# Another order of the background work in the scans of two Mamba layers

## The chip, the cores and the metric

The kernel runs on one core of one Trainium2 chip. The metric is the device time of one execution in microseconds; the median of three runs is given. The core has five engines, each with a queue of its own that it works off in order: TensorE (PE, matmuls into PSUM), VectorE (DVE), ScalarE (ACT, functions from tables that have to be loaded), GpSimd (POOL), and SyncE (SP), which here issues the DMAs.

## The reference

Four images go through four layers with residual connections. Two are attention layers, which the change doesn't touch. The third is a Mamba layer, the fourth a grouped Mamba layer with an MLP. What the last two compute, cut to what matters:

```python
# Mamba: xn is the normalised input, B=4, L=4096, D_INNER=512, 16 states
xi, z = split(xn @ in_proj.T)
u     = silu(causal_conv4(xi) + conv_b)
dt, Bm, Cm = split(u @ x_proj.T)                 # "x_proj"
delta = softplus(dt @ dt_proj + dt_proj_b)       # "delta"
h_t   = exp(delta_t * A) * h_{t-1} + (delta_t * u_t) * B_t     # 16 states
y_t   = sum_n h_t[n] * C_t[n]
out   = ((y + u * D) * silu(z)) @ out_proj.T

# grouped layer: the 256 channels in 4 groups of 64, each its own Mamba (128 inner channels,
# shared weights); then for every group
m = ln(mamba(group)); m = gelu(m @ fc1 + b1) @ fc2 + b2 + skip * group     # "MLP"
y = silu(batchnorm(outc @ concat(m)))                                       # "out_conv", "out_silu"
```

## The kernel before, in words

The images are worked off one after the other, the layers of an image too. A Mamba layer's 4096 time steps are cut into four chunks (k) of 1024. In a chunk there are four blocks of 128 inner channels. For the Mamba layer these are the blocks d = 0 to 3. For the grouped layer they are the four groups, taken as two pairs (c = 0, 1); the pair's first block is `even`, its second `odd`. A block has 16 slots, one for each state n. So a layer has 256 slots.

`scan_blocks` writes out, slot by slot, what each engine gets. In slot i:

- VectorE multiplies `du` with the spread B (L913, tile `pb`) and runs the scan (L919, `h`).
- GpSimd multiplies h with C (L925, `hc`). Two slots ahead it makes the product `du*B` (L830, `bb`) for "apart" slots, in which VectorE then doesn't multiply. Apart are slots 0, 4, 8 of a grouped block and 0, 5, 10 of a Mamba block. B for them comes by DMA, loaded four slots ahead.
- ScalarE makes exp(delta*A) three slots ahead (L856, `da`; for apart slots `dap` two slots ahead, into PSUM) and keeps the state (L861).
- TensorE spreads B over the partitions two slots ahead (L844, `pb`) and adds up y by transposes (L872, `y`) for the slot before.
- In between come the slot's background steps, `blk["bg"][n]`, in the order in which `put` filed them.

On TensorE the background of slot i stands ahead of the spread for slot i+2 and of the transposes of slot i-1. On VectorE it stands behind the scan of slot i, on GpSimd behind `hc` of slot i, on ScalarE behind `da` for slot i+3. What waits in the background thus holds up what stands behind it on its engine.

The background prepares what later blocks need, in the grouped layer:

- `x_proj` (`table_steps`): two projections with their evictions (x0, x1: L1623, L1072; behind the second the DMAs that store B and C), then four steps that split the table into two bf16 parts: a cast on ScalarE (L1080), a subtraction of 64 rows on GpSimd ("r64", L1083), a second cast, a subtraction of 32 rows ("r32"). The steps are numbered 0 to 5. For the Mamba layer each projection is two steps (0 to 3), and the parts are 4 to 7.
- `delta` (`delta_steps`): matmul and three functions on ScalarE (softplus, L1040 to L1044), an add on VectorE (L1048), the same for the second half, then `times_u` on GpSimd (L1052, `du`).
- `norm`: mean, center (L979), deviation (L990, L953), scale (GpSimd, L996), affine (ScalarE, L1003) for each half of the next chunk.
- `mlp`: out_proj (L1638), deviation (L1648), scale (GpSimd, L1653), hidden(0) (L1659), fc1 (gelu with two table loads, L1666, and hidden(1)), fc2(0), fc2(1) (L1682, L1687). m0 and m1 are the two halves of the pair before.
- `out_conv` (L1707, L1713), `out_silu`, `out` (GpSimd add L1732 and DMA); `all_u` (L1570) and `silu` (L1602, two table loads) make u for the next pair; `in_z` makes z.

All these matmuls share a PSUM pool, "mm", of two banks; hidden takes both. `end` finishes a block in slots 1 to 3 of the next one (L883 copy of y, L893 and L897 `fin_ps`, L886). Lists named `late` pass steps on to the next pair; what is left after the last pair runs behind the scan, in the tail, ahead of the last pair's MLP.

For the Mamba layer the change concerns the last block (d = 3) of each chunk but the last, in which u's last quarter, x_proj and the first delta of the next chunk are made.

Of the kernel before, what the change touches and what calls it, by code (L numbers as in the profile page):

```python
# [45 lines left out]
class Net:  # L46
# [1065 lines left out]
    def mamba_layer(self, x, bridge, pe_dram, w_in, w_cw, w_x, w_dt, w_out, v_dram):  # L1112
        tc, nc = self.tc, self.nc
        ND = 4
        with ExitStack() as ctx:
# [226 lines left out]
            for k in range(n_chunk):  # L1342
# [28 lines left out]
                if more:  # L1371

                    if k == 0:
                        put(0, (0,), (lambda: begin(1),))
                        put(0, (0, 0, 1, 3, 4, 5, 6, 7), self.later(lambda: norm(1, 0), 8))
                    h1 = self.later(lambda k=k: norm(k + 1, 1), 8)
                    if k:
                        put(0, (2, 4, 5, 7, 8, 13, 14, 15), h1)
                    else:
                        put(0, (7, 8, 9, 12, 13, 14, 15), h1[:7])  # L1380
                        put(1, (1,), h1[7:])
                    if k + 2 < n_chunk:
                        put(3, (3,), (lambda k=k: begin(k + 2),))
                        h0 = self.later(lambda k=k: norm(k + 2, 0), 8)
                        put(3, (4, 6, 7, 14, 15), h0[:5])
                        chunks[k + 1]["late"] = ((0, 1, 2), h0[5:])
                    if k:
                        put(0, *chunks[k]["late"])
                    u = all_u(k + 1)
                    put(1, range(5, 16), u[:11])  # L1390
                    put(2, range(14), u[11:25])
                    put(3, (1, 2, 3, 4, 5, 5, 6), u[25:])
                    xs = x_proj(k + 1)
                    put(2, (13,), (silu((k + 1, 0, "u"), (k + 1, 1, "u"), (k + 1, 2, "u"),
                                        (k, 2, "zs")),))
                    put(3, (7,), (silu((k + 1, 3, "u"), (k, 3, "zs")),))
                    put(3, (7, 8, 8, 9, 9, 10, 11, 12), xs)
                    put(3, (9, 10, 10, 11, 12), delta(k + 1, 0))
                else:
                    put(2, (13,), (silu((k, 2, "zs"), (k, 3, "zs")),))  # L1400

                    sums, about, square, squares, early_squares = stats

                    def square_into(i):
                        tag, bufs = ("pe", 1) if i % 2 else ("u", 5)
                        square(i, work.tile([P, NC], F32, tag=tag, name="cs_sq", bufs=bufs))

                    for i in range(6):
                        put(1 + (13 + i) // DS, ((13 + i) % DS,), (lambda i=i: sums(i),))
                        put(2 + (12 + i) // DS, ((12 + i) % DS,), (lambda i=i: square_into(i),))  # L1410
                        put(2 + (13 + i) // DS, ((13 + i) % DS,), (lambda i=i: squares(i),))
                    put(2, (3,), (about,))
                    put(3, (3,), (early_squares,))
                    for i in range(4):
                        at = (6 + 2 * i, 7 + 2 * i)
                        put(3, at, out_proj(k, i // 2, i % 2, ((0, 1, 2),)))
# [70 lines left out]
    def grouped_mamba_layer(self, x, bridge, begun, ws_dram, outc_dram, v_dram, out_b):  # L1487
        tc, nc = self.tc, self.nc
        w_in, w_cw, w_x, w_dt, w_out, w_f1, w_f2 = ws_dram
        with ExitStack() as ctx:  # L1490
# [136 lines left out]
            def delta(k, q):  # L1627
                return self.delta_steps(chunks[k]["blocks"][q], wdt, work, psum)
# [188 lines left out]
            for i, (k, c) in enumerate(pairs):  # L1817
# [12 lines left out]
                if more:  # L1830
                    h0, h1 = (self.later(lambda k=k, s=s: norm(k + 1, s), 5) for s in range(2))
                    put(even, (0,), (lambda k=k: begin(k + 1),))
                    put(even, (0, 1, 4, 5, 6), h0)
                    put(even, (14, 15), h1)
                    put(odd, (1, 2, 3), h1[2:])
                put(even, (4, 5, 6, 7, 8, 9), x_proj(k, 2 * c + 1))
                if i:
                    m0, m1 = mlp(*pairs[i - 1], 0), mlp(*pairs[i - 1], 1)
                    put(even, (5, 6, 7, 10, 11, 12, 13), m0)
                    put(even, (6, 7, 8), m1)  # L1840
                    if c == 0:
                        put(even, (14, 15), m1[3:])
                        put(odd, (0, 1), m1[5:])
                    else:
                        put(odd, (15,), m1[3:])
                        late.append(((0, 1, 1), m1[4:]))
                put(even, (7, 8, 8, 9, 10), delta(k, 2 * c + 1))
                also = [lambda k=k: out_silu(k - 1)] if c == 1 and k else []
                if i == 0:
                    put(even, (0,), xs0[5:])  # L1850
# [6 lines left out]
                if c == 1 and k:  # L1857
                    put(even, (4, 4, 5, 5), [out(k - 1, *sm) for sm in outs])
                if c == 0 and k:
                    put(odd, (10, 12, 15), [out_conv(k - 1, *sm) for sm in outs[:3]])  # L1860
                    late.append(((0,), [out_conv(k - 1, *outs[3])]))

                if i + 1 < len(pairs):
                    nk, ncol = pairs[i + 1]
                    put(odd, (4, 5, 6, 7), all_u(nk, ncol))
                    put(odd, (7,), (silu(nk, ncol, "u"),))
                    put(odd, (8, 8, 8, 9, 10, 11), x_proj(nk, 2 * ncol))
                    put(odd, (9, 10, 10, 11, 12), delta(nk, 2 * ncol))
                    put(odd, (13, 14), [in_z(nk, ncol, s) for s in range(2)])
            self.scan_blocks(  # L1870
                [blk for c in chunks for blk in c["blocks"]], loop, psum, psb, psy, (0, 4, 8),
# [125 lines left out]
```

## Time and profile before

| what | us |
|---|---|
| median of 3 runs (lowest to highest) | 12572.97 (12561.93 to 12574.42) |
| the profiled execution: device time, span | 12578.04, 12576.3 |
| Mamba scan, second image | 968.9 |
| between the two scans | 58.8 |
| grouped scan, second image | 980.9 |
| tail behind it, to the end of the image | 56.4 |
| busy over the whole span: PE, DVE, ACT, POOL | 10378.1, 10244.0, 7241.3, 9022.1 |

An image is some 3140 us: two attention layers (about 1080), the Mamba scan, the grouped scan. In the rows of a time line the columns are start, length, engine, line, operation, out<-in, shapes and count; the bracket at the end is the idle time of the engine just before, and what ended it. In rows of groups the columns behind the bar are busy us and mean ns of one, then idle us before them with what ended it.

### The profile page before, as it was taken

The numbers are of one execution on the slowest core, as the hardware profiler recorded it, in microseconds if no ns is written. First come the engines' busy times: TensorE is split into PE (matmuls) and PEld (weight loads), VectorE is DVE, ScalarE is ACT, GpSimd is POOL, SyncE is SP. The second block draws the span as 40 slices with busy tenths as digits, with TensorE's granted clock in tenths as the row PEclk, the third lists the DMA queues.
The fourth block names the chain that finished last, engine by engine and source line by source line (L and its number), as shares of the span: only waits on it lengthen the run. The fifth ranks groups of instructions, "written<-read, shape, count | busy, mean of one in ns | idle before, by whom it ended". The sixth has DMA issues, their size and how long they took to land. (4 is left out here: it accounts for less than half of the span.)

```text
span 12576.3 us, 159645 instructions
## 1 busy us (share of the span) xinstructions
PE 10378.1 (83%) x54656; PEld 6079.4 (48%) x54656; DVE 10244.0 (81%) x9074; ACT 7241.3 (58%) x13292; POOL 9022.1 (72%) x4634
## 2 busy tenths in 40 slices
PE   8987887777898788778789878877778987887787
PEld 4664444443466454444446645444434664444443
DVE  6778997887677899798767789978976778997897
ACT  4565554776456555477646655547764565554776
POOL 4666886887466688688746668868874666886887
PEclk9998998998899899899889989989988998998998
DMA  3343444554334455455433445445543344554554
GB/s 96 106 130 129 171 168 137 168 169 141 98 107 126 132 169 169 137 170 169 141 98 108 127 133 170 168 137 169 169 141 97 107 128 131 171 168 138 169 168 142
DMA packets 687147, 1782.94 MB, mean 142 GB/s; under 512 B 89856, under 2 KB 197888, under 8 KB 685312
## 3 DMA queue, kind: packets, MB, share of 16 engines
q1 hardware_dynamic: 686336, 1772.74, 43.6%
q8 instruction: 435, 7.13, 0.2%
q14 instruction: 376, 3.08, 0.1%
HBM read 1610.91 MB, written 94.37 MB: 136 GB/s over the span
## 5 line engine op out<-in xcount | busy, mean ns | idle before, releaser
L925 POOL TENSOR_TENSOR hc<-h,cb 128x1024 f32<-128x1024 f32 x2056 | 4817.5, 2351 | 1099.0 <-DVE h L919 502.8
L919 DVE TENSOR_TENSOR_SCAN h<-da,m_state,pb 128x1024 f32<-128x1024 f32 x1248 | 2920.4, 2340 | 162.0 <-DVE pb L913 1.9
L872 PE MATMUL y<-ident,hc 128*128 128x128 f32 x16384 | 2378.0, 294 | 313.7 <-POOL hc L925 211.4
L872 PEld LDWEIGHTS y<-ident,hc 128*128 128x128 f32 x16384 | 2098.8, 152 | 979.4 <-POOL hc L925 374.5
L913 DVE TENSOR_TENSOR pb<-du,pb 128x1024 f32<-128x1024 f32 x1672 | 2025.8, 1212 | 147.3 <-PE pb L844 98.8
L856 ACT ACTIVATE da<-delta,m_v 128x1024 f32<-128x1024 f32 x1672 | 1899.1, 1141 | 215.9 <-DVE h L919 205.4
L844 PE MATMUL pb<-m_parts,pick 128*128 128x512 bf16 x3280 | 1082.2, 414 | 896.9 <-DVE h L919 893.7
L502 ACT ACTIVATE pr<-sc,mn 128x256 f32<-128x256 f32 x2048 | 956.7, 478 | 783.9 <-PE pt_ps L528 560.7
L514 POOL TENSOR_TENSOR pr<-pr,sm 128x1024 f32<-128x1024 f32 x512 | 967.8, 1896 | 572.3 <-DVE sm L512 392.4
L844 PEld LDWEIGHTS <-pick 128*128 128x128 bf16 x3280 | 253.0, 101 | 1884.2 <-DVE h L919 1226.5
L919 DVE TENSOR_TENSOR_SCAN h<-da,pb 128x1024 f32<-128x1024 f32 x424 | 969.7, 2287 | 55.5 <-DVE pb L913 1.4
L830 POOL TENSOR_TENSOR bb<-du,bb 128x1024 f32<-128x1024 f32 x376 | 888.7, 2363 | 71.8 <-DMA bb<-m_cd 65.2
L491 DVE TENSOR_REDUCE mn<-sc 128x4 f32<-128x1024 f32 x512 | 610.0, 1219 | 257.4 <-PE sc L480 256.0
L919 DVE TENSOR_TENSOR_SCAN h<-dap,m_state,bb 128x1024 f32<-128x1024 f32 x288 | 672.1, 2334 | 80.4 <-ACT dap L856 67.7
L528 PE MATMUL pt_ps<-ident,pr 128*128 128x128 f32 x4096 | 572.3, 283 | 144.5 <-ACT pts L541 64.2
L208 PE MATMUL conv_ps<-att_y,att_wb 128*128 128x512 f32 x1536 | 688.8, 593 | 0.0
L856 ACT ACTIVATE dap<-delta,m_v 128x1024 f32<-128x1024 f32 x376 | 419.6, 1116 | 457.7 <-DVE h L919 349.1
L552 PE MATMUL ov_ps<-pts,kv 128*64 128x128 f32 x8192 | 595.9, 294 | 91.1 <-DVE vimg L565 74.6
L480 PE MATMUL sc<-kv,q 64*128 64x128 f32 x8192 | 575.6, 289 | 81.4 <-DMA kv<-kv_dram 58.6
L528 PEld LDWEIGHTS pt_ps<-ident,pr 128*128 128x128 f32 x4096 | 466.5, 144 | 314.1 <-issue 152.2
L480 PEld LDWEIGHTS sc<-kv,q 64*128 64x128 f32 x8192 | 518.3, 197 | 124.6 <-issue 46.5
L552 PEld LDWEIGHTS ov_ps<-pts,kv 128*64 128x64 f32 x8192 | 468.1, 144 | 216.3 <-DVE vimg L565 131.1
(263 smaller groups left out, 18265.0 us busy)
## 6 DMA issues: line engine op xcount, KB each, us to landing
cb<-m_cd SPq DMA_DIRECT2D x2048, 512.0 KB, 3.8
kv<-kv_dram SPq DMA_DIRECT2D x2048, 128.0 KB, 2.6
bb<-m_cd SPq DMA_DIRECT2D x376, 512.0 KB, 5.1
q<-q SPq DMA_DIRECT2D x256, 256.0 KB, 3.9
kv_dram<-kst SPq DMA_DIRECT2D x128, 256.0 KB, 3.5
kv_dram<-vn SPq DMA_DIRECT2D x128, 256.0 KB, 3.6
x<-in_x_dram SPq DMA_DIRECT2D x8, 2048.0 KB, 10.7
m_pe<-in_pe_dram SPq DMA_DIRECT2D x32, 512.0 KB, 5.2
```

The costliest lines, as they stand in the source:

```text
L480: nc.tensor.matmul(sc[w][:, r, cq, :], qbuf[sj % 2][m][rows, b, 2 * a + w].rearrange("p h t -> p (h t)"), t[rows, :, k0 : k0 + 64], start= ...
L502: nc.scalar.activation(t[:, cq].rearrange("p j r t -> p r j t"), sc[w][:, :, cq, :].rearrange("p r (j t) -> p r j t", j=2), AF.Exp, bias=m ...
L514: nc.gpsimd.tensor_tensor(t, t, s.rearrange("p (a o) -> p a o", o=1).to_broadcast([P, 4, 256]), ALU.mult,)
L528: nc.tensor.transpose(pt[w][j][:, cq, :], t[:, cq, j].rearrange("p r t -> p (r t)"), self.ident,)
L552: nc.tensor.matmul(ov[i][b * 64 : b * 64 + 64, m, :, :, w, :], t[:, j, c0 : c0 + 64], pts[w][j][:, cq, :], start=(j == 0), stop=(j == 1),)
L830: nc.gpsimd.tensor_tensor(pb[i], slots[i][0]["du"], pb[i], ALU.mult)
L844: nc.tensor.matmul(pb[i][:, ss], self.pick[:, n : n + 1].to_broadcast([P, P]), blk["parts"][:, ss], start=True, stop=True,)
L856: nc.scalar.activation(da[i], blk["delta"], AF.Exp, scale=blk["a"](n))
L872: nc.tensor.matmul(blk["y"][:, ss], t[:, ss], self.ident, is_transpose=True, start=(n == 0 and ss.start % NT == 0), stop=(n == DS - 1 and ...
L913: nc.vector.tensor_tensor(pb[i], blk["du"], pb[i], ALU.mult)
L919: nc.vector.tensor_tensor_scan(h[i][:, ss], da[i][:, ss], pb[i][:, ss], state, ALU.mult, ALU.add)
L925: nc.gpsimd.tensor_tensor(hc[i][:, ss], h[i][:, ss], cb[i][:, ss], ALU.mult)
```

## The change

Three places are edited, all of them lists of slots.

```diff
 # Mamba layer, last block of a chunk
-                    put(3, (7, 8, 8, 9, 9, 10, 11, 12), xs)
-                    put(3, (9, 10, 10, 11, 12), delta(k + 1, 0))
+                    put(3, (7, 8, 8, 9), xs)
+                    put(3, (10, 11, 11, 12, 12), delta(k + 1, 0))
+                    put(3, (10, 11, 12, 13), xs[4:])
 # grouped layer, even block of a pair
-                    put(even, (0, 1, 4, 5, 6), h0)
+                    put(even, (0, 1, 12, 13, 14), h0)
                     put(even, (14, 15), h1)
-                    put(odd, (1, 2, 3), h1[2:])
-                put(even, (4, 5, 6, 7, 8, 9), x_proj(k, 2 * c + 1))
+                    put(odd, (3, 4, 5), h1[2:])
+                xs, ds = x_proj(k, 2 * c + 1), delta(k, 2 * c + 1)
+                put(even, (4, 5), xs)
+                put(even, (7, 8, 8, 9, 9) if c else (6, 7, 7, 8, 9), ds)
+                put(even, (9, 10, 12, 13), xs[2:])
                 if i:
                     m0, m1 = mlp(*pairs[i - 1], 0), mlp(*pairs[i - 1], 1)
-                    put(even, (5, 6, 7, 10, 11, 12, 13), m0)
-                    put(even, (6, 7, 8), m1)
-                    if c == 0:
-                        put(even, (14, 15), m1[3:])
-                        put(odd, (0, 1), m1[5:])
-                    else:
-                        put(odd, (15,), m1[3:])
-                        late.append(((0, 1, 1), m1[4:]))
-                put(even, (7, 8, 8, 9, 10), delta(k, 2 * c + 1))
+                    put(even, (9, 10, 11), m1)
+                    put(even, (8, 9, 9, 10, 11, 12, 12), m0)
+                    put(even, (15,), m1[3:])
+                    put(odd, (0, 1, 1), m1[4:])
 # grouped layer, odd block of a pair
-                    put(odd, (10, 12, 15), [out_conv(k - 1, *sm) for sm in outs[:3]])
+                    put(odd, (3, 8, 9), [out_conv(k - 1, *sm) for sm in outs[:3]])
                     late.append(((0,), [out_conv(k - 1, *outs[3])]))
-                    put(odd, (8, 8, 8, 9, 10, 11), x_proj(nk, 2 * ncol))
-                    put(odd, (9, 10, 10, 11, 12), delta(nk, 2 * ncol))
+                    xs = x_proj(nk, 2 * ncol)
+                    put(odd, (8, 9), xs)
+                    put(odd, (10, 11, 11, 12, 12), delta(nk, 2 * ncol))
+                    put(odd, (10, 11, 12, 13), xs[2:])
```

`put(block, slots, steps)` files the steps one by one under the slots of the list; what is left over on either side is dropped there. So in the Mamba layer delta goes a slot later, and the table's parts go behind it (10 to 13 instead of 9 to 12). In the grouped layer's even block delta keeps slots 7 to 9 where c is 1 and goes to 6 to 8 where c is 0, with `times_u` in slot 9; the parts go from slots 6 to 9 to slots 9 to 13; the MLP of the pair before starts in slot 8 instead of 5, with both fc2 steps of its first half in slot 12; the first half of the next chunk's norm has its last three steps in slots 12 to 14 instead of 4 to 6. The MLP's second half always has hidden(0) in slot 15 of the even block and the rest in slots 0 and 1 of the odd one; before, this was slots 14 and 15 and then 0 and 1 for c = 0, and slot 15 of the odd block and the next pair for c = 1. For the last pair that rest was done in the tail. In the odd block x_proj takes a slot for each projection, delta and the parts go a slot or two later, and three of the four out_conv steps go from slots 10, 12, 15 to 3, 8, 9.

## The prediction

> **What bounds the kernel now.** I read the page first, then the busy time by stretch for the second of the four images, then VectorE's groups within one stretch, then time lines of single engines.
>
> ```profile
> 4229.70:5198.60 968.90, 805.54 (x3486) 466.72 (x3487) 903.10 (x559) 502.86 (x730) 799.40 (x353) 0.92 0.50 168
> 5257.40:6238.30 980.90, 766.81 (x3492) 424.28 (x3490) 874.04 (x531) 655.82 (x951) 851.52 (x386) 0.88 0.49 165
> 6238.30:6294.70 56.40, 37.83 (x98) 13.37 (x98) 1.38 (x2) 29.79 (x40) 11.22 (x12) 0.81 0.07 24
> ```
>
> Columns: stretch, its length, then busy us of PE, PE's weight loads, DVE, ACT, POOL, the granted clock, DMA share, GB/s. The rows are the 256 scan slots of the Mamba layer, those of the grouped layer, and the tail behind them. In both scans VectorE is the bound (903 of 969, 874 of 981 us); a slot costs it 1.21 (multiply) and 2.34 (scan), 3.6 us with its gaps, or 2.24 where GpSimd does the multiply. So only VectorE's 66 and 107 idle us, and the tail, can be won. The same again for each image (grouped scans of 982, 981, 980 and 978 us).
>
> ```profile
> L919 DVE TENSOR_TENSOR_SCAN h<-da,m_state,pb 128x1024 f32<-128x1024 f32 x156 | 365.0, 2340 | 20.1 <-ACT dap L856 0.5
> L913 DVE TENSOR_TENSOR pb<-du,pb 128x1024 f32<-128x1024 f32 x208 | 251.8, 1211 | 28.3 <-PE pb L844 17.1 <-PE pb L838 10.9
> L1048 DVE SCALAR_TENSOR_TENSOR delta<-dt_ps,delta 128x512 f32<-128x512 f32 x30 | 20.5, 684 | 32.2 <-ACT delta L1044 32.2
> ```
>
> These are the grouped scan's groups. 32.2 us are the add L1048 waiting for ACT's softplus; 17.1 the multiply waiting for PE's spread (L844). The 20.1 before L919 is the fixed 0.13 per slot.
>
> ```profile
> 5600.95 1.28 ACT L1602 ACT_TABLE_LOAD   x1
> ...
> 5604.25 1.28 ACT L949 ACT_TABLE_LOAD   x1
> 5605.55 1.15 ACT L856 ACTIVATE da<-delta,m_v 128x1024 f32<-128x1024 f32 x1
> ...
> 5606.70 1.25 ACT L1072 ACTIVATE m_bct<-x_ps,ident 128x512 f32<-128x512 f32 x2
> 5607.97 1.06 ACT L1080 ACTIVATE m_parts<-m_bct 128x1024 bf16<-128x1024 f32 x1
> 5608.94 1.15 ACT L856 ACTIVATE da<-delta,m_v 128x1024 f32<-128x1024 f32 x1
> ...
> 5610.09 0.57 ACT L1042 ACTIVATE delta<-dt_ps 128x512 f32<-128x512 f32 x1
> ...
> 5611.35 0.63 ACT L1044 ACTIVATE delta<-delta 128x512 f32<-128x512 f32 x1
> ```
>
> ```profile
> 5612.02 0.69 DVE L1048 SCALAR_TENSOR_TENSOR delta<-dt_ps,delta 128x512 f32<-128x512 f32 x1 [2.41 <-ACT delta L1044]
> ```
>
> Block 5 (I number blocks 4k+2c+odd): ACT runs without a gap from the silu's table load, is a whole slot behind, and the add at the head of VectorE's queue stops the scan for 2.41 us.
>
> **The change, part by part.** Engine by engine the number of each instruction stays the same; only the order changes. S(n) is the end of scan n-1.
>
> *Mamba, blocks 3, 7, 11.* Waits of the first add: 2.04, 1.85, 3.11, and 0.72 for GpSimd's product at the start of block 12. The softplus's first half goes from slot 9 to 10, its add from 10 to 11, the cast L1080 behind it. In block 11 the projection's matmul would run 18.3 to 19.4 us behind S(6), ACT's three steps (0.6+0.66+0.63) to 21.3; the add's turn comes at 20.85: 0.45 remains. GpSimd's subtractions move a slot back (r64 2.1 us, r32 2.1); counted on from S(10) its product for the next block ends 0.3 late there, and hides under the norm's centring (1.1) in 3 and 7. Gain 7.7-0.8 = 6.9 per image.
>
> *Tail.* Before, the last block leaves fc1 and fc2 of one half for after the scan; its first hidden matmul, issued in slot 15, holds both "mm" banks:
>
> ```profile
> 6243.54 1.12 PE L893 MATMUL fin_ps<-ident,du 128*128 128x128 f32 x4 [3.21 <-ACT hid L1666]
> ...
> 6248.86 1.98 PE L1659 MATMUL f_ps<-m_sq,m_wf 64*128 64x512 f32 x4
> ...
> 6253.60 2.06 PE L1638 MATMUL m_ps<-m_zs,m_wout 128*64 128x512 f32 x8
> ```
>
> After, fc1 and fc2 stand in slots 0 and 1 of block 15. The final transposes start behind the first copy of y, at about 6241.0; two of 0.6+1.0 each; out_proj starts at about 6244.2 instead of 6253.6. Gain 9.4, I take 9. If ACT were not free there, the two table loads (2.56) would be the loss.
>
> *Odd blocks with c=0 (5, 9, 13).* Waits before in block 5: 2.18+0.87 for the spread in slots 1 and 2 (PE stands behind fc1's gelu), 2.41+0.27 for the adds: 5.7. With gelu in slot 0 and fc2 in slot 1 they become what block 4 shows today for that order, 0.6 (fin_ps). x_proj now follows slot by slot (8, 9), out_conv beside it (8, 9; 0.66 ACT each). ACT counted on from the silu's end (12.6 us behind S(6)): decay and copy 1.15, out_conv 0.66, x 0.57, the same again, decay 1.15, matmul, softplus: done at 20.4; the add's turn is 20.5. The second half of x waits on PE for its bank: 0.25 late. Gain 4.6 each, 13.8. Block 1 has no out_conv, waits 2.74+0.95: gain 3. The two DMAs that store B and C follow x's second half, a slot later; the load that needs them is in slot 12. SP's queue is otherwise passed by nothing.
>
> *Even, c=0 (4, 8, 12).* Before 1.77+0.61. The add moves to slot 7, after which ACT is ready 3 us early: no wait. But all of m0's scale (1.24) now stands on GpSimd in slot 9 behind hc (2.31) and times_u (2.31): from S(10)=34.5 it ends at 40.4. PE reaches hidden(0) at 37.1 and waits; behind it waits the spread of slot 12. hidden 1.1, spread 0.6: 42.1 against S(12)=41.7: 0.45 late. If PE runs at half clock after that idle time, 2.08+1.04: 1.8 late. Block 4 today shows exactly these slow rows (hidden 2.08, spread 1.04) after 3.98 idle, so I take 1.7 on average: gain 0.7 each, 2.1. GpSimd's queue to the next block's product is then 22.8 us against VectorE's 21.6, not later than the scan that has slipped by 1.7.
>
> *Even, c=1 (2, 6, 10; 14 without norm).* Block 6 waits 4.24+2.17+0.40. ACT loses n0's deviation and affine and the MLP's squares ahead of the softplus, so ACT's share goes; n0's scale (1.96 us on GpSimd) passes from ahead of the output adds to behind hc of slot 13; the product L830 still comes behind four output adds (1.23 each) on GpSimd, 1.2 late. New: hidden(0) 0.8 late; slot 12 now holds norm deviation (2.75 on PE), fc2 both (2.9), spread and turn (1.6): counted from hidden(1), which ends 1.8 behind S(12), the spread ends S(12)+9.55 against S(14)=S(12)+7.2: 2.35 late. oc3 and the norm's mean start later by GpSimd's backlog: 1.2. Sum 5.55 with a fast PE (gain 1.2), 13.8 with a slow one from slot 7 on:
>
> ```profile
> 5658.56 1.09 PE L872 MATMUL y<-ident,hc 128*128 128x128 f32 x8
> 5662.77 2.07 PE L1648 MATMUL m_pv<-m_sq,one_half 128*128 128x512 f32 x2 [3.12 <-ACT m_sq L1643]
> 5664.78 2.07 PE L1040 MATMUL dt_ps<-m_bct,m_wdt 64*128 64x512 f32 x2
> ```
>
> This is the same place before: after 3.12 us idle each fp32 matmul takes 2.07, and a hot one takes 1.02; the granted clock is 0.56 in the 13 us that follow. After the change I find 2.9 us of idle there. I take a loss of 1.5 for 6 and 10, a gain of 1.5 for 2 (no output yet), 1 for 14: in all -0.5.
>
> [...]
>
> *Odd, c=1 (3, 7, 11).* Before 2.5 to 3.1. fc1 in slot 0, fc2 in slot 1 (0.6); n1's deviation, scale, affine three slots to two slots later: 2.75 PE in slot 3 (0.4), affine on ACT waits for GpSimd, so u's second half and the silu come 2.3 later (0.75 on the spread, 1.2 at the add). About 3.0: gain 0; bounds -3 and +2.5. Blocks 15 and 0: -0.3 and -0.5.
>
> Sum per image: 6.9+9+13.8+3+2.1-0.5+0-0.8 = 33.5; four images 134. The profiled execution took 12578.0 (span 12576.3), 5 over the median 12572.97, so 12573-134 = 12439 us.
>
> **Rivals.** (1) *The waits move only within the grouped scan*: what the adds give back, hidden(0), slot 12 and GpSimd's backlog take. For it: POOL is busy 852 of 981 us. Mamba and tail remain: 4 x 15.9 = 64, 12509. (2) *All named waits vanish*: grouped waits over 0.3 from block 1 on sum to about 60 us per image; with 16.4 it is 76, four times 305: 12270; half of the 60 still 12390. Against it: slot 12's sum. (3) *Slower: PE becomes the bound of the even blocks* because hidden(0) and m1's deviation stand in PE's queue ahead of the spread and wait for GpSimd's scale, PE falls to half clock there and meets slot 12 slow. It costs 7 in each of six even blocks beyond what they lose today, 2.5 in each of three odd: 49.5 against 32.7 won elsewhere, +67: 12640. It decides from about 4.2 us per even block. For it the 2.07 rows; against it that in block 4 the slow rows last only 5 us.
>
> **Numbers.** Forecast 0.54, rival (1) 0.22, (2) 0.12, (3) 0.12. The range runs from 12350, short of rival (2)'s end, over (1) to 12565. Faster by over 0.2% (25 us, about what these times can tell) 0.80, within 0.2% 0.08, slower 0.12.
>
> **What would show it.** Right: L1048's idle time in a grouped scan falls from 32 to under 8 us, in Mamba's from 8.7 to about 3; the tail from 56.4 to 47; no 2-us wait in slot 1 of blocks 5, 9, 13. New waits before L913 in slots 12 and 14 of even blocks, released by PE's spread. Wrong: an L1048 wait as before, a tail still above 53, or long waits before the slot-0 scan for L830.

## The result, and the profile after

| | before | after |
|---|---|---|
| median, us (lowest to highest, 20 runs each) | 12569.67 (12561.42 to 12577.31) | 12593.13 (12586.01 to 12605.56) |
| ratio | | 1.002, 95% interval 1.0013 to 1.0026 |
| span of the profiled execution | 12576.3 | 12589.2 |
| the four Mamba scans | 968.4, 968.9, 969.3, 968.5 | 959.7, 958.6, 960.0, 960.0 |
| the four grouped scans | 982.1, 980.9, 980.4, 978.5 | 999.6, 1000.1, 998.2, 1001.3 |
| from the end of a grouped scan to the next Mamba scan; behind the last | 1137, 1132, 1135; 56 | 1124, 1130, 1129; 51 |

The change makes the kernel 0.2% slower; 12439 was forecast. In the profiled executions the Mamba scans give 36.9 us, the stretches behind the grouped scans 26, and the grouped scans take 77.3. Behind the Mamba edit each line of the changed kernel has a number one higher than before (L1707 becomes L1708, L1659 becomes L1660); lines ahead of it, such as L1048, keep theirs. The busy time by stretch of the changed kernel, second image (columns as before):

```profile
4222.60:5181.30 958.70, 795.21 (x3486) 459.67 (x3487) 902.86 (x559) 502.35 (x730) 799.25 (x353) 0.94 0.51 170
...
5240.40:6240.50 1000.10, 767.37 (x3504) 422.86 (x3503) 878.57 (x531) 662.10 (x958) 851.02 (x386) 0.89 0.48 162
6240.50:6291.50 51.00, 35.22 (x88) 13.12 (x86) 1.42 (x3) 23.82 (x33) 11.44 (x13) 0.77 0.08 26
```

VectorE does the same work in the grouped scan (878.6 us, 874.0 before) and idles 15 us more (121.5 against 106.9). Its groups there tell for whom it waits:

```profile
L913 DVE TENSOR_TENSOR pb<-du,pb 128x1024 f32<-128x1024 f32 x208 | 252.7, 1215 | 64.0 <-PE pb L844 52.8 <-PE pb L838 10.9
...
L1048 DVE SCALAR_TENSOR_TENSOR delta<-dt_ps,delta 128x512 f32<-128x512 f32 x30 | 20.2, 673 | 6.7 <-ACT delta L1044 6.7
...
L979 DVE TENSOR_TENSOR m_xn<-x,ln_pm 128x1024 f32<-128x1024 f32 x6 | 7.3, 1209 | 7.4 <-PE ln_pm L976 7.4
```

The change does what it is built to do: the add's wait for the softplus falls from 32.2 to 6.7 us. But the multiply's wait for PE's spread (L844) rises from 17.1 to 52.8, and the norm's centring L979, which had 0.9 per image before (mean of four), now has 7.4. PE's clock isn't worse: 0.89 against 0.88. The mean length of the blocks 0 to 15 over the four images, each counted from the end of the last scan of the block before, says where:

```
before 73.1 58.9 62.8 59.4 58.6 62.2 63.9 60.8 58.7 62.3 63.7 60.7 58.7 61.2 60.4 55.1
after  72.1 57.2 62.7 62.2 58.4 62.4 69.0 62.2 58.2 62.7 69.5 61.8 57.4 62.8 64.0 57.4
```

Blocks 6 and 10 lose 5.1 and 5.8, 14 loses 3.6; 3, 7, 11 lose 2.8, 1.4, 1.1; 13 and 15 lose 1.6 and 2.3. Three places can be read at once. First block 5 of the second image, the place of the prediction's 2.41 us wait (time line, PE's and VectorE's rows):

```profile
5591.99 1.98 PE L1708 MATMUL oc_ps<-xo,m_woc 128*128 128x512 f32 x4 [1.72 <-ACT yo L1714]
5593.81 1.02 PE L1624 MATMUL x_ps<-m_u,m_wx 128*128 128x512 f32 x2
5594.67 0.59 PE L844 MATMUL pb<-m_parts,pick 128*128 128x512 bf16 x2
```

```profile
5589.43 1.23 DVE L913 TENSOR_TENSOR pb<-du,pb 128x1024 f32<-128x1024 f32 x1 [0.91 <-PE pb L844]
5591.36 2.35 DVE L919 TENSOR_TENSOR_SCAN h<-da,m_state,pb 128x1024 f32<-128x1024 f32 x1 [0.70 <-ACT m_state L861]
5595.30 1.23 DVE L913 TENSOR_TENSOR pb<-du,pb 128x1024 f32<-128x1024 f32 x1 [1.59 <-PE pb L844]
...
5599.18 0.69 DVE L1048 SCALAR_TENSOR_TENSOR delta<-dt_ps,delta 128x512 f32<-128x512 f32 x1 [0.17 <-ACT delta L1044]
```

The add waits 0.17 instead of 2.41. But out_conv's matmul for slot 9 waits 1.72 us for the bank that ACT empties only behind the silu, the projection and the spread stand behind it, and the scan loses 1.59, after 0.91 and 0.70 a slot earlier: 3.2 us in slots 10 and 11. Slots 2 to 4 of blocks 5, 9 and 13 wait 1.9, 2.8 and 2.9 us in this image, for the spread behind the MLP's steps and for the end of the block before.

Second the end of block 6, in which the prediction counted norm deviation, skip and fc2 in slot 12 (time line of PE, then VectorE's row):

```profile
5670.34 1.88 PE L990 MATMUL ln_pv<-ln_sq,one_ln 128*128 128x512 f32 x4
5672.06 1.02 PE L991 MATMUL ln_pv<-m_wi,one_ln 128*128 128x512 f32 x2
5672.92 1.02 PE L1683 MATMUL f_ps<-m_xn,m_skip 128*128 128x512 f32 x2
5673.87 1.94 PE L1688 MATMUL f_ps<-hid,m_wf 128*64 128x512 f32 x8
5675.74 0.61 PE L844 MATMUL pb<-m_parts,pick 128*128 128x512 bf16 x2
```

```profile
5676.38 1.23 DVE L913 TENSOR_TENSOR pb<-du,pb 128x1024 f32<-128x1024 f32 x1 [3.01 <-PE pb L844]
```

The stack is as foreseen; the wait is 3.01 where 2.35 was worked out.

The third place is the tail (PE's rows, the changed kernel, then e6, one of the kernels below, whose tail has the same program):

```profile
6243.79 1.12 PE L893 MATMUL fin_ps<-ident,du 128*128 128x128 f32 x4 [0.74 <-ACT du L883]
6244.70 1.92 PE L897 MATMUL fin_ps<-m_u,diag_d 128*128 128x512 f32 x2
...
6248.93 1.94 PE L1639 MATMUL m_ps<-m_zs,m_wout 128*64 128x512 f32 x8
```

```profile
6194.81 0.66 PE L893 MATMUL fin_ps<-ident,du 128*128 128x128 f32 x4 [0.74 <-ACT du L883]
6195.31 1.02 PE L897 MATMUL fin_ps<-m_u,diag_d 128*128 128x512 f32 x2
...
6197.56 1.94 PE L1639 MATMUL m_ps<-m_zs,m_wout 128*64 128x512 f32 x8
```

In the changed kernel the transposes start 3.3 us behind the scan's end (2.7 worked out), but on a slow PE: 1.12 and 1.92 instead of 0.6 and 1.0. out_proj starts 8.4 behind the scan's end, not 5.9. In e6 PE is fast here in all four images: out_proj starts 6.0 behind the scan's end, and the last tail takes 47.7 (47 was forecast).

### The profile page after: what moved, and what is told of

Read it like the earlier page. It is cut to its first block, busy times and chain, and to the rows that moved or that the text cites. A ratio compares the mean times of both kernels' runs of the same rounds, so it can differ in the third digit from the quotient of the medians.

```text
span 12589.2 us, 159740 instructions
## 1 busy us (share of the span) xinstructions
PE 10337.2 (82%) x54656; PEld 6053.7 (48%) x54656; DVE 10261.4 (82%) x9074; ACT 7237.2 (57%) x13292; POOL 9019.8 (72%) x4634
## 3 DMA queue, kind: packets, MB, share of 16 engines
q14 instruction: 375, 3.07, 0.1%
## 5 line engine op out<-in xcount | busy, mean ns | idle before, releaser
L844 PE MATMUL pb<-m_parts,pick 128*128 128x512 bf16 x3280 | 1077.7, 413 | 908.8 <-DVE h L919 865.7
L844 PEld LDWEIGHTS <-pick 128*128 128x128 bf16 x3280 | 261.9, 101 | 1893.7 <-DVE h L919 1028.8
L919 DVE TENSOR_TENSOR_SCAN h<-dap,m_state,bb 128x1024 f32<-128x1024 f32 x288 | 673.0, 2337 | 61.3 <-POOL bb L830 31.2
L480 PE MATMUL sc<-kv,q 64*128 64x128 f32 x8192 | 571.9, 288 | 82.2 <-DMA kv<-kv_dram 66.1
```

The costliest lines, as they stand in the source:

```text
L480: nc.tensor.matmul(sc[w][:, r, cq, :], qbuf[sj % 2][m][rows, b, 2 * a + w].rearrange("p h t -> p (h t)"), t[rows, :, k0 : k0 + 64], start= ...
L844: nc.tensor.matmul(pb[i][:, ss], self.pick[:, n : n + 1].to_broadcast([P, P]), blk["parts"][:, ss], start=True, stop=True,)
L919: nc.vector.tensor_tensor_scan(h[i][:, ss], da[i][:, ss], pb[i][:, ss], state, ALU.mult, ALU.add)
```

## The experiments

Eighteen kernels were run, each timed beside the kernel before, whose medians lay between 12567.3 and 12570.4. The ratios are to it. Kernels from e5 on contain the Mamba edit and the last pair's MLP inside the scan, unless it says "after". The intervals are some 10 to 20 us wide to either side, so a difference of some 15 us between two of these kernels is weak evidence; single executions of e5 and e7, whose medians lie 13 apart, overlap.

| run | what it is | median, us | ratio (95% interval) |
|---|---|---|---|
| e1 | before + Mamba edit | 12534.4 | 0.9972 (0.9962 to 0.9983) |
| e4 | before + last pair's m1 inside the scan | 12544.5 | 0.9979 (0.9969 to 0.9989) |
| e5 | both | 12499.2 | 0.9942 (0.9925 to 0.9959) |
| e6 | e5 + odd order | 12472.8 | 0.9923 (0.9907 to 0.994) |
| e7 | e5 + even order | 12512.3 | 0.9953 (0.9936 to 0.997) |
| e8 | e5 + norm | 12481.2 | 0.9928 (0.9911 to 0.9944) |
| e10 | e5 + m1's slots | 12535.4 | 0.9974 (0.9964 to 0.9984) |
| e11 | e5 + even order + norm | 12547.3 | 0.9984 (0.9974 to 0.9993) |
| e12 | e5 + odd order + norm | 12505.3 | 0.995 (0.9934 to 0.9967) |
| e13 | e6 + norm's first half only | 12474.5 | 0.9921 (0.9905 to 0.9938) |
| e14 | e13 + m1's slots where c = 0 | 12453.5 | 0.9908 (0.9892 to 0.9925) |
| e16 | e5 + odd + even order | 12518.4 | 0.9955 (0.9938 to 0.9971) |
| e15 | e16 + norm's first half, fc2 both in slot 12 | 12519.5 | 0.9956 (0.994 to 0.9973) |
| e9 | e15 + norm's second half = after without m1's slots and out_conv | 12534.8 | 0.9974 (0.9965 to 0.9984) |
| e2 | after, out_conv as before | 12571.1 | 1.0002 (0.9993 to 1.0012) |
| e3 | after, slot 12 unstacked | 12595.1 | 1.0021 (1.0011 to 1.0031) |
| e17 | after, r64 a slot earlier in odd blocks | 12610.6 | 1.003 (1.0019 to 1.004) |
| e18 | e14, r64 a slot earlier in odd blocks | 12455.5 | 0.991 (0.9893 to 0.9926) |

**e1, the Mamba edit alone.** The kernel before with the first hunk of the change.

> The kernel before with the Mamba layer's edit alone. If the prediction's Mamba step holds, each Mamba scan shortens by 7 to 10 us and nothing else moves: 28 to 40 us less than before, 12530 to 12545. If the traces' shorter Mamba scans were an effect of the other edits, no difference beyond 10 us.

Its Mamba scans took 960.6, 960.2, 961.9 and 960.2: the 34 us of the time are all there, and this part of the change is independent of the rest.

**e4, the tail alone.** The kernel before, in which only the last pair's second half goes inside the scan:

```diff
+                        if i + 1 < len(pairs):
                             put(odd, (15,), m1[3:])
                             late.append(((0, 1, 1), m1[4:]))
+                        else:
+                            put(even, (15,), m1[3:])
+                            put(odd, (0, 1, 1), m1[4:])
```

> The kernel before with the last pair's second MLP half finished inside the last block (hidden in slot 15 of block 14, the rest in slots 0 and 1 of block 15) instead of behind the scan. The prediction's step said 9 us shorter a tail; the changed kernel's trace shows 5.5 shorter and block 15 longer by 2.7. If that is all of it, 3 us an image, 10 to 15 us less than before; if the tail's 9 were lost to something else of the change, up to 36 less.

The whole is 24 us shorter, 6 per image. The last tail is 51.7, 4.7 shorter, and the stretches from a grouped scan to the next Mamba scan are 1128, 1134 and 1127: 20 us with the tail, and 3 in the grouped scans.

**e5, both.** 

> The kernel before with the Mamba layer's edit and the last pair's MLP half inside the last block, the grouped blocks else as before. The two alone gave 34 and 24 us; they touch different stretches, so the sum, 58 less: about 12510. The changed kernel, which has both, would then lose some 83 us in the rest of the grouped scan.

12499.2, 71 below the kernel before, and so 14 more than the two added up (-34 and -24), which is about the width of the intervals. All that follows is measured against it; the rest of the change, which is the grouped scan's, thus costs 94.

**e2 and e3, two suspects in the changed kernel.** e2 puts three out_conv steps back; e3 takes the norm out of slot 12 and one fc2 to slot 13:

```diff
 # e2
-                    put(odd, (3, 8, 9), [out_conv(k - 1, *sm) for sm in outs[:3]])
+                    put(odd, (10, 12, 15), [out_conv(k - 1, *sm) for sm in outs[:3]])
 # e3
-                    put(even, (0, 1, 12, 13, 14), h0)
+                    put(even, (0, 1, 4, 5, 6), h0)
-                    put(even, (8, 9, 9, 10, 11, 12, 12), m0)
+                    put(even, (8, 9, 9, 10, 11, 12, 13), m0)
```

> The changed kernel with out_conv back in slots 10, 12, 15 of the odd blocks. Theory A (PE's queue: steps that wait for one of the two PSUM banks stand ahead of the spread): the waits before L913 in slots 10 and 11 of blocks 5, 9 and 13 (0.9 and 1.6 to 2.1 us) fall to under 1 us in sum, two to three us a block, 25 to 35 us less than the changed kernel. Rival B (GpSimd's backlog holds the transposes and so the spread): GpSimd's order is untouched, so these waits stay and the time is within 10 us of the changed kernel's.

> The changed kernel with the first norm half's deviation, scale and affine back in slots 4, 5, 6 and the last fc2 step in slot 13. Theory A: the 3.0 us wait in slot 14 of blocks 2, 6 and 10 goes, 36 us; some 1 to 2 us a block come back at slot 8 or 9 because ScalarE gets 3 us of work ahead of the softplus; net 15 to 35 us less than the changed kernel. Rival B: GpSimd's scale (2 us) leaves slot 13, which would shorten the wait before slot 0 of the next block instead and leave slot 14 as it is. Rival C (PE at half clock): slots 10 to 13 keep their 0.5 to 1 us waits, whatever is moved.

e2 is 22 us below the changed kernel; blocks 5, 9, 13 shrink from 62.4, 62.7, 62.8 to 60.3, 61.3, 61.0. So out_conv's new slots cost these blocks 1.4 to 2.1 us each: in block 5 of the second image the 3.2 us in slots 10 and 11 fall to 0.4, and the add in slot 12 waits 1.1 instead. e3 gains nothing: the wait of 3.01 in slot 14 is gone, but in its place the product for slot 8 is late by 3.2 us instead of 1.25. A stack on PE's path was taken away, and GpSimd's queue took its place.

**e6, e7, e8: the three reorderings one at a time on e5.**

```diff
 # e6, odd order
-                    put(odd, (8, 8, 8, 9, 10, 11), x_proj(nk, 2 * ncol))
-                    put(odd, (9, 10, 10, 11, 12), delta(nk, 2 * ncol))
+                    xs = x_proj(nk, 2 * ncol)
+                    put(odd, (8, 9), xs)
+                    put(odd, (10, 11, 11, 12, 12), delta(nk, 2 * ncol))
+                    put(odd, (10, 11, 12, 13), xs[2:])
 # e7, even order: x_proj, delta and m0, m1 as in the change, but m0 to (8, 9, 9, 10, 11, 12, 13)
 # e8, norm
+                    put(even, (0, 1, 12, 13, 14), h0)
+                    put(odd, (3, 4, 5), h1[2:])
```

> The kernel of e5 with the odd blocks' x_proj one projection a slot and softplus and table parts later, as in the change, out_conv in its old slots. Theory A: what the prediction said of odd blocks: L1048's 2.4 to 2.5 us waits there go and 0.5 to 1 us come back (PE waiting for a bank), 1.5 to 2.5 us for each of seven blocks, 40 to 65 us less than e5. Rival B (GpSimd's backlog): r64 and r32 now stand ahead of the product for the next block; slot 0 and the start of the next even block give back 1.5 us or more a block, so less than 20 us are left.

> The kernel of e5 with the even blocks' softplus, table parts and MLP in the order of the change (fc2 in slots 12 and 13, norm in its old slots). Theory A: L1048's waits of 1.3 to 2.2 us in these go, but hidden(0) behind GpSimd's scale, and a product for slot 8 that is late by 3 us in blocks 2, 6, 10, take them: within 25 us of e5. Rival B: GpSimd's work in slots 9 to 14 is what costs, so this alone shows the changed kernel's loss: 40 us or more over e5.

> The kernel of e5 with only the next chunk's norm moved (first half's deviation, scale, affine in slots 12 to 14, second half's in slots 3 to 5 of the odd block). GpSimd and ScalarE are relieved ahead of slot 8 of blocks 2, 6, 10: the wait there (3.2, 4.2, 4.2 us) falls to about 1.3 and the add's (2.2) shrinks. Given back: 0.9 in slot 5 of the odd block and some in slot 13 or 14. Theory A: 2 to 4 us for each of three blocks, 25 to 45 us less than e5. If the stack of PE work in slots 12 to 15 costs more than slot 8 gains, no gain or a loss.

Alone they give -26, +13 and -18. In e6 the L1048 wait of blocks 5, 9, 13 is gone, but the even blocks from 2 on are 1.7 to 3.1 longer than in e5: a part of what the odd block gains is given back a block later. In e7 block 6 loses the 4.2 us wait before its slot-8 scan only to wait 3.2 there for GpSimd's product. In e8 that wait falls to 1.3.

**e9 to e12: which pieces harm each other.** e9 is e2 with m1 as in e4; e10 is e5 with `put(even, (15,), m1[3:])` and `put(odd, (0, 1, 1), m1[4:])` for every pair; e11 is e7 and e8, e12 is e6 and e8 together.

> The changed kernel with out_conv in its old slots, as in e2 (12571), and besides with the MLP's second half as before (slots 14, 15 and then 0, 1 where c is 0; slot 15 of the odd block and the next pair where c is 1; only the last pair's inside the scan, as in e4). If the second half's early place is what the sum of the single parts (12499 -26 +13 -18 = 12468) lacks against 12571: about 12470 to 12500. If it is not, and even blocks and norm harm each other: 12555 to 12590.

> e5 with nothing but the change's slots for the MLP's second half (hidden in slot 15 of every even block, the rest in slots 0 and 1 of the odd one). If that place costs by itself: 12560 to 12600, with the loss in blocks 1, 3, 7, 11 where PE waits for gelu ahead of the spread and u comes late. If it only costs beside a late first half: within 15 us of 12499. My forecast in the prediction had it a small gain: 12480.

> e5 with the even blocks' new order and the norm's new slots together, the second half of the MLP as before, fc2 in slots 12 and 13. Alone they gave +13 and -18. If they add up: 12494. If they harm each other in slots 12 to 14 and in the next block's product behind GpSimd's backlog: 12540 to 12590.

> e5 with the odd blocks' softplus a slot later (e6, -26) and the norm later (e8, -18), out_conv and even blocks as before. If they add up: 12455, the best of all. If both load GpSimd in the same blocks (r64, r32 and the norm's scale): 12470 to 12490.

The times of e9 and e10 lie between the outcomes that I expected. The slots of the MLP's second half cost 36 us twice over: e2 against e9, and e10 against e5. In e2 against e9 blocks 3, 7 and 11 are 2.0 to 2.6 longer and blocks 5, 9 and 13 1.5 to 3.0. Against e5, e10's blocks 3, 7 and 11 are 4.4, 5.5 and 4.8 longer (means 64.8, 66.1, 65.4), and its blocks 5, 9, 13 are 1.5, 1.0 and 1.4 shorter. Block 7 in e10's time line (PE's rows, VectorE's below):

```profile
5683.10 1.88 PE L990 MATMUL ln_pv<-ln_sq,one_ln 128*128 128x512 f32 x4
5684.82 1.02 PE L991 MATMUL ln_pv<-m_wi,one_ln 128*128 128x512 f32 x2
5685.68 1.02 PE L1683 MATMUL f_ps<-m_xn,m_skip 128*128 128x512 f32 x2
5686.63 1.94 PE L1688 MATMUL f_ps<-hid,m_wf 128*64 128x512 f32 x8
```

```profile
5689.14 1.23 DVE L913 TENSOR_TENSOR pb<-du,pb 128x1024 f32<-128x1024 f32 x1 [3.01 <-PE f_ps L1688]
```

Blocks 3, 7 and 11 are the ones that hold the second half of the norm. Before, the MLP's last steps stood a block later, where there is no norm; now both stand in slot 1, 5.9 us of PE ahead of one spread. (In the changed kernel the norm's second half stands two slots later, so the two don't meet in this way.) e11 and e12 show a second harm: the norm, a gain of 18 alone, costs 35 on top of e7 and 32 on top of e6.

**e13 to e16: which half of the norm, and what is left.** e13 is e6 with only `put(even, (0, 1, 12, 13, 14), h0)`; e14 adds m1's new slots for c = 0 alone; e15 is e9 with `put(odd, (1, 2, 3), h1[2:])`; e16 is e6 and e7 together.

> e6 with only the first half of the norm moved (slots 12 to 14 of the even block), its second half left in slots 1 to 3 of the odd one. If the second half's move is what turns e6's gain and the norm's into a loss (e12: 12505 instead of 12455), because it makes u and with it the softplus late in blocks 3, 7, 11: 12430 to 12460. If it is the first half, by GpSimd's scale behind hc: 12490 to 12510.

> e13 and besides the MLP's second half as in the change where c is 0 alone (hidden in slot 15 of the even block, the rest in slots 0 and 1 of the odd one, blocks 5, 9, 13). In e10 these blocks became 1.3 us shorter and blocks 3, 7, 11, where c is 1, 4.9 longer. If the loss comes from meeting the norm's second half, which only the latter hold: 10 to 20 under e13. If the place itself costs: 10 to 40 over it.

> e9 (the changed kernel with out_conv and the MLP's second half as before; 12535) with the norm's second half back in slots 1 to 3 of the odd block. If that half is the harmful one: 12490 to 12510, by 2 us in each of blocks 3, 7, 11. If not: 12525 to 12545.

> e6 and e7 together, norm as before, fc2 in slots 12 and 13. Alone -26 and +13 against e5 (12499): 12486 if they add up. From e9, e11 and e12 a remainder of -36 falls to this pair or to the two fc2 steps in slot 12: 12450 if it is the pair.

The second half of the norm is the harmful one: moving it costs 31 beside the odd order (e12 against e13) and 15 in e9 against e15. The time of e15 lies between the two outcomes expected, so this half is a part of the loss there and not the whole. Its three slots make u's second half late, and in e12 blocks 3, 7 and 11 wait for the spread in slot 5 (up to 2.2) and slot 10 (up to 2.3), as the prediction had it. The first half gave nothing on e6, where a gain was expected. e14 is 21 below e13, as expected if the MLP's place does no harm where no norm stands. But its trace doesn't place the gain there: blocks 5, 9 and 13 change by +1.4, -0.8 and -1.2, and of the 26 us between the two profiled executions some 13 lie in the grouped scans and 16 behind them. The even order beside the odd one costs 46 (e16 against e6), alone 13; the -36 that I looked for in this pair were not there.

A part of what the two orders do to each other stands at the start of blocks 6 and 10. The kernel before, block 10 (GpSimd, PE):

```profile
5873.50 2.37 POOL L830 TENSOR_TENSOR bb<-du,bb 128x1024 f32<-128x1024 f32 x1
...
5878.23 1.09 PE L872 MATMUL y<-ident,hc 128*128 128x128 f32 x8 [0.34 <-POOL hc L925]
5879.16 1.88 PE L1707 MATMUL oc_ps<-xo,m_woc 128*128 128x512 f32 x4
```

The changed kernel, the same place (GpSimd, PE, VectorE):

```profile
5862.20 2.12 POOL L1083 TENSOR_TENSOR m_parts<-m_bct,m_parts 32x1024 bf16<-32x1024 f32 x1
5864.29 2.35 POOL L830 TENSOR_TENSOR bb<-du,bb 128x1024 f32<-128x1024 f32 x1
5866.61 6.94 POOL L925 TENSOR_TENSOR hc<-h,cb 128x1024 f32<-128x1024 f32 x3
```

```profile
5866.63 1.01 PE L844 MATMUL pb<-m_parts,pick 128*128 128x512 bf16 x2 [3.25 <-POOL bb L830]
5869.00 1.97 PE L872 MATMUL y<-ident,hc 128*128 128x128 f32 x8 [1.35 <-POOL hc L925]
5870.76 3.11 PE L1708 MATMUL oc_ps<-xo,m_woc 128*128 128x512 f32 x4
```

```profile
5864.14 2.35 DVE L919 TENSOR_TENSOR_SCAN h<-da,m_state,pb 128x1024 f32<-128x1024 f32 x1
...
5875.62 1.22 DVE L979 TENSOR_TENSOR m_xn<-x,ln_pm 128x1024 f32<-128x1024 f32 x1 [3.00 <-PE ln_pm L976]
```

The table's last part, r32, now stands on GpSimd directly ahead of the product for the next block; the product and the multiplies behind it end 1.5 us later against the block's start. PE waits 1.35 us for them, where it waited 0.34. Ahead of that it idles 3.25 instead of 0.89. The bracket names the product, but the spread starts at 5866.63, before the product ends (5866.64), and 0.14 us behind the end of the scan of slot 15 (5866.49). That scan reads the one of the pool's two `pb` tiles that this spread writes next; in e6 and e16 below it starts 0.14 us behind that scan too, and the bracket names the scan. This wait is longer because out_conv, 1.88 us of PE in slot 15 before, has gone to slot 9: in e2, which has it back, it is 1.54. So out_conv's move leaves PE idle here, and GpSimd's backlog adds the rest. Then PE runs at half clock (0.53 granted over the next 7 us): the same transposes take 1.97 instead of 1.09, out_conv 3.11 instead of 1.88. The norm's mean is behind these, and VectorE waits 3.00 for it. The same in two kernels that differ only in the even order, first e6, then e16 (GpSimd, PE, VectorE, block 10):

```profile
5829.51 2.34 POOL L830 TENSOR_TENSOR bb<-du,bb 128x1024 f32<-128x1024 f32 x1
...
5831.61 0.38 PE L844 MATMUL pb<-m_parts,pick 128*128 128x512 bf16 x1 [1.29 <-DVE h L919]
5834.20 1.09 PE L872 MATMUL y<-ident,hc 128*128 128x128 f32 x8 [2.22 <-POOL hc L925]
5835.13 1.88 PE L1708 MATMUL oc_ps<-xo,m_woc 128*128 128x512 f32 x4
```

```profile
5838.77 1.22 DVE L979 TENSOR_TENSOR m_xn<-x,ln_pm 128x1024 f32<-128x1024 f32 x1 [0.93 <-PE ln_pm L976]
```

```profile
5847.00 2.34 POOL L830 TENSOR_TENSOR bb<-du,bb 128x1024 f32<-128x1024 f32 x1
...
5849.10 0.59 PE L844 MATMUL pb<-m_parts,pick 128*128 128x512 bf16 x2 [1.30 <-DVE h L919]
5851.70 1.97 PE L872 MATMUL y<-ident,hc 128*128 128x128 f32 x8 [2.00 <-POOL hc L925]
5853.46 3.62 PE L1708 MATMUL oc_ps<-xo,m_woc 128*128 128x512 f32 x4
```

```profile
5859.00 1.22 DVE L979 TENSOR_TENSOR m_xn<-x,ln_pm 128x1024 f32<-128x1024 f32 x1 [3.68 <-PE ln_pm L976]
```

GpSimd stands alike in both against the scan, PE waits nearly alike; once it stays fast (granted clock 1.00 over the next 7 us) and once not (0.61), and that is 2.75 us on the path. Each trace has eight such places (blocks 6 and 10, four images). out_conv's first matmul there was slow (over 0.9 us) in none of them in before, e5, e7, e8, e10 and e11, which have the odd order of before; in those with the new one it was slow in 1 (e6), 3 (e13, e18), 4 (e2, e14), 5 (e15), 6 (e9), 7 (e12) and 8 (e3, e16, e17, after). Seven more slow places at 2.75 us are 19 of the 46 us between e6 and e16. Blocks 6 and 10 are 3.1 and 3.4 longer in e16; so is block 1, by 3.1, and block 15, by 2.0. What these two lose was not followed.

**e17 and e18: GpSimd's queue shortened.** In the changed kernel and in e14:

```diff
-                    put(odd, (10, 11, 12, 13), xs[2:])
+                    put(odd, (9, 10, 12, 13), xs[2:])
```

> The changed kernel with one thing altered: in the odd blocks the table's first cast and GpSimd's r64 stand a slot earlier (slots 9, 10 instead of 10, 11), so that r64 goes into the time in which GpSimd has none of its queue left, and the rest of its queue at the end of the block is 2.1 us shorter. If GpSimd's queue there makes PE wait for hc, fall to half clock and hold the norm's mean (slot 2 of blocks 6 and 10, 2.53 and 3.00): these waits fall below 1 us and out_conv's matmuls at the start of block 6 and 10, slow in all eight, are fast in most; against that the softplus loses up to 1 us in each odd block behind the cast: 12570 to 12585. If those waits have another cause: 12595 to 12620.

> The same in e14 (12453.5), in which four of these eight places are slow. With GpSimd as the cause: 12435 to 12455, by the slow places that go and the 0.6 and 0.4 us before the slot-0 scans, less the cast ahead of the softplus. Otherwise: 12460 to 12480.

e17 is 17 us slower than the changed kernel, which is the outcome that I had put down to another cause than GpSimd. The waits in slot 2 of blocks 6 and 10 are still there (2.3 to 2.8), and PE idles 3.25 and 1.34 us ahead of them as before the edit. GpSimd's rows at the end of block 9 in e17, behind VectorE's scan, say why:

```profile
5869.77 2.35 DVE L919 TENSOR_TENSOR_SCAN h<-da,m_state,pb 128x1024 f32<-128x1024 f32 x1
...
5872.25 2.36 POOL L925 TENSOR_TENSOR hc<-h,cb 128x1024 f32<-128x1024 f32 x1 [2.53 <-issue]
5874.57 2.35 POOL L1052 TENSOR_TENSOR du<-delta,m_u 128x1024 f32<-128x1024 f32 x1
...
5879.18 2.13 POOL L1083 TENSOR_TENSOR m_parts<-m_bct,m_parts 32x1024 bf16<-32x1024 f32 x1
5881.28 2.35 POOL L830 TENSOR_TENSOR bb<-du,bb 128x1024 f32<-128x1024 f32 x1
```

Where r64 stood there is now a hole of 2.53 us: the scan whose `h` this `hc` takes ends at 5872.12, and from there `du`, r32 and the product follow as before. The queue is counted from that hole on, and I had moved a step ahead of it. So the edit didn't shorten what it was to shorten, and it doesn't settle what GpSimd's part is; in all eight places PE was slow again. What r32 alone is worth, and what out_conv's place in slot 15 alone is worth, was not tried. e18 is within 2 us of e14.

The best kernel run is e14: 12453.5, 0.9% under the kernel before. Its VectorE groups in the grouped scan of the second image:

```profile
L913 DVE TENSOR_TENSOR pb<-du,pb 128x1024 f32<-128x1024 f32 x208 | 251.7, 1210 | 28.0 <-PE pb L844 16.9 <-PE pb L838 10.9
...
L1048 DVE SCALAR_TENSOR_TENSOR delta<-dt_ps,delta 128x512 f32<-128x512 f32 x30 | 20.3, 675 | 16.2 <-ACT delta L1044 16.2
```

Half of the softplus's wait is gone here, and the wait for the spread is 16.9, as before (17.1), instead of 52.8. It leaves the even blocks' order, the norm's second half and out_conv where they were.

## Why the prediction was wrong, point by point

From e5 to the changed kernel the steps can be walked one by one: odd and even order +19 (e16), the norm's first half and both fc2 steps in slot 12 +1 (e15), the norm's second half +15 (e9), the MLP's second half +36 (e2), out_conv +22 (after). Before rounding that is 94. The smaller of these differences are about as wide as the intervals, and the order of the walk matters, since the pieces are not additive: the odd order is a gain of 26 on its own, and the norm one of 18.

By the blocks of the profiled executions, per image (gain in us):

| part | forecast | measured |
|---|---|---|
| Mamba | 6.9 | 9.2 |
| tail and stretches behind the grouped scans | 9 | 6.5 |
| odd, c=0: 5, 9, 13 | 13.8 | -2.2 |
| block 1 | 3 | 1.7 |
| even, c=0: 4, 8, 12 | 2.1 | 2.0 |
| even, c=1: 2, 6, 10, 14 | -0.5 | -14.4 |
| odd, c=1: 3, 7, 11 | 0 | -5.3 |
| blocks 15 and 0 | -0.8 | -1.3 |

*Mamba.* Right in mechanism: L1048 waits 3.0 there instead of 8.7, and the wait for GpSimd's product in block 12 is gone, where 0.3 was left in the sum. e1 alone gave 8.5 per image.

*Tail.* The step that failed is "two of 0.6+1.0 each": PE ran them at half clock (1.12 and 1.92, granted clock 0.52 over the 5.1 us up to out_proj; the row of the kernel before that the prediction shows has 1.12 too), which is 1.9 of the 2.5 us by which out_proj starts late. The last tail became 5.4 shorter. With a fast PE the forecast comes out (e6: 47.7), so the path was right and the clock on it was not.

*Odd c=0.* This is the largest miss of the sum, 16 us per image. The wait at the add went as worked out, and the blocks gained nothing: -0.2, -0.4 and -1.6. The first failed step is "the second half of x waits on PE for its bank: 0.25 late"; 3.2 came in slots 10 and 11. I followed ACT's queue to the softplus, but not the bank of out_conv in slot 9 back to ACT's copy behind the silu, with the spread behind it on PE: 1.72 us, and 0.9 and 0.7 in the slot ahead (e2: 22 us in all). The second is the 0.6 for the MLP's steps in slots 0 and 1, taken over from block 4; 1.9 to 2.9 came in slots 2 to 4. With both put back (e9) these blocks are 3.2 to 3.4 us shorter than before.

*Even c=1.* Here the blocks lost most against the kernel before: 6 and 10 lost 5.1 and 5.8, 14 lost 3.6, and 2 gained 0.1. The 1.2 before slot 8 came (1.25). "ACT's share goes" failed: the add still waits 1.77 in slot 10. hidden(0) was in the sum with 0.8; 0.5 to 1.0 came in each of slots 11 to 13. The norm's mean was in it with 1.2; 2.5 to 3.0 came in slot 2, on a slow PE. For that term I had followed r64 and r32 on GpSimd for the Mamba layer alone, not for blocks 5 and 9, and had not asked what PE does in slot 15 once out_conv has left it. In slot 12 the stack was sized rightly, and that the wait was near is in part luck: hidden(1) ended 4.5 us behind S(12) instead of 1.8, but the scans had slipped by 1.6 as well.

*Odd c=1.* Each step was priced, and most came dearer (second image): the MLP's steps 1.4 to 2.8 in slots 1 to 4 (0.6 in the sum), the norm 0.9 in slot 5 (0.4), u's second half 1.5 to 1.6 on the spread in slot 10 (0.75); the 1.2 at the add did not come. e10 shows a dearer meeting of the MLP with the norm in its old slots, 4.4 to 5.5 per block.

*Block 1, 4, 8, 12, 15 and 0.* Blocks 4, 8 and 12 gained 0.2, 0.5 and 1.3 (0.7 each). The slow PE that was foreseen there came in full in block 4 alone, in three of the four images:

```profile
5535.29 2.08 PE L1660 MATMUL f_ps<-m_sq,m_wf 64*128 64x512 f32 x4 [3.59 <-POOL m_sq L1654]
```

hidden(0) waits for GpSimd's scale, PE is slow (granted clock 0.50 over the 3 us from this row on), and slot 12 loses 1.97 (1.8 worked out). In blocks 8 and 12 it waits 2.5 to 3.3 and takes 1.13 in seven of eight cases, and in these slot 12 loses 0.6 to 0.7 (0.45 worked out with a fast PE); in the eighth it takes 1.59, and the slot loses 1.48. Block 0 gained 1.0 (-0.5), block 15 lost 2.3 (-0.3). The last pair's m1 is not what it loses by (e4: 0.2); e7 has most of it, with 57.1 for this block.

*What would show it.* Four of the five signs came: L1048 below 8 and at 3, no wait of 2 us in slot 1 of blocks 5, 9, 13, the new waits in slots 12 and 14; only the tail stayed at 51. None of the three signs of being wrong came. They were signs that the old waits go, and said nothing of what comes for them.

*The rivals.* What came is rival (1) carried past zero: the waits moved within the grouped scan, and more came than went. Rival (3) named an event that came, PE idle and then at half clock, but mostly in another place: ahead of slot 12 in block 4, not in block 6, where hidden(0) waited 0.70 us, and at the start of blocks 6 and 10, where only a part of the idle time is GpSimd's. Its price, 7 us in each of six even blocks, doesn't fit: eight places at some 2.7 us are 22 us in all four images.

*PE's clock.* Rows of nearly equal idle time disagree: 1.3 and 2.0 us gave slow rows in all eight places of e16 and in three of e13, 1.3 and 2.2 us in one of e6, six of e9 and seven of e12. In the kernel before, 3.12 us in block 6 (2.07 for two fp32 matmuls) and 3.98 in block 4 (1.04 for the spread) gave slow rows, and 3.07 in Mamba block 11 a fast one:

```profile
4954.22 0.61 PE L844 MATMUL pb<-m_parts,pick 128*128 128x512 bf16 x2 [3.07 <-DVE h L919]
```

Over the 7 us from that row on the granted clock was 0.58 even so. In the changed kernel 3.31 us ahead of hidden(0) in block 8, more than the 3.12, gave a fast row (1.13 for four matmuls). What decides beside the idle time, no run shows.

## What to carry to other kernels

When a step is moved off one wait, follow each of its instructions to the end of its new queue, and the step that stood there too: here the add's wait fell by 25 us in the second image, and 36 came back before the multiply, in waits for another engine. Two moves that are each free can be dear together when they end in one slot ahead of the same instruction: list what stands ahead of each spread after all moves, not after each. Where a change has parts that don't touch (here the Mamba edit and the tail, -71), measure them alone: they hid that the rest cost 94. A step that is moved away also leaves a gap: out_conv had kept PE busy for 1.88 us in slot 15.

## What the runs showed of the hardware

The idle time alone didn't tell whether PE fell to half clock. At the start of block 10 it idled 1.30 and 2.00 us, with 0.6 us of work between them, in e16, and had a granted clock of 0.61 over the next 7 us: eight transposes took 1.97 instead of 1.09 us, four fp32 matmuls 3.62 instead of 1.88. In e6 it idled 1.29 and 2.22 us there and had 1.00. Idle times of 3.6 us ahead of hidden(0) in block 4 of the changed kernel gave slow rows in three images of three (2.08 us for its four matmuls, granted clock 0.50 over 3 us); after 2.76 us in the fourth they took 1.13. After 2.5 to 3.3 us there, in blocks 8 and 12, they took 1.13 in seven cases of eight, and 1.59 in the eighth; the granted clock over the 7 us from their start was 1.00 in three of the eight and 0.76 in five. The mean clock of the scan hides this: 0.89 in the changed kernel, 0.88 before, with 19 us more in the scan. In the rows shown the half clock cost time where something that VectorE waited for stood behind it: the norm's mean in blocks 6 and 10 (waits of 2.53 and 3.00 us in the second image), the spread in block 4 (1.97).
